# Layer 1's output stores issued from ScalarE, its loads alone on SyncE's queue, and eight matrix buffers

## The chip, the core and the metric

The kernel runs on one core of a Trainium2 chip. A core has a matrix engine (TensorE, PE in the profile), three engines for elementwise work (VectorE or DVE, ScalarE or ACT, GpSimd or POOL) and SyncE (SP), which here only issues transfers between the chip's main memory and its on-chip memory. ScalarE can issue transfers too; each of the two has a queue of its own. [...]

The metric is the device time of one execution in microseconds (us). Before the change it is 4470.12 us, the median of three runs between 4469.93 and 4470.48.

## The reference, cut to what matters

Two layers follow each other. Layer 0 takes the image through two 2-D Fourier transforms, a mixing of channels and a 3x3 convolution; the change doesn't touch it. Layer 1 filters along the first image axis:

```python
def _L1_conv_ref(x, w_real, w_imag):            # x: (4, 256, 256, 64)
    trend = _moving_average(x, 25)              # along axis 1
    xf = jnp.fft.rfft(x - trend, axis=1)
    xs = xf[:, :128]
    ys = jnp.einsum('bmnc,cmk->bknc', xs, w_real + 1j * w_imag)
    yf = jnp.concatenate([ys, zeros], axis=1)
    return trend + jnp.fft.irfft(yf, n=256, axis=1)
```

All of this is linear along axis 1 and differs only by channel. So it is one 256x256 matrix for each of the 64 channels, applied to 4 images of 256x256 values. The kernel makes the 64 matrices early, beside the first stages of layer 0, and puts them in main memory (`m_d`).

## The kernel before

Layer 0 ends with its result in main memory (`x2_d`). Layer 1 then works in 16 steps: eight groups of eight channels (`c`), and in each group two halves of the batch (`b0`). I call such a step, eight channels of two images, a half group.

```python
CM, CO = 2, 2
BH = max(1, B // 2)                    # 2 images
# CG = 8 channels, N = 256, P = 128, SW = 16

def x2_load(pool, c, b0, bufs):        # four loads of 1024 KB
    xc = pool.tile([P, 2, BH, N // SW, CG, SW], F32, tag="xc", name=..., bufs=bufs)
    for b in range(BH):
        for t in range(2):
            nc.sync.dma_start(xc[:, t, b], x2_d[b0 + b, t * P : (t + 1) * P, c // CG])
    return xc

def matrix_load(pool, c):              # the matrices of two channels, 512 KB
    mt = pool.tile([P, CM, 2, N], F32, tag="mt", name=f"mt_{c}", bufs=6)
    nc.sync.dma_start(mt, m_d[c : c + CM].rearrange("c p t n -> p c t n"))
    return mt

def layer1(c, b0, mts, xc, pool):
    nf = BH * N
    for i in range(CG):
        if i % CO == 0:
            oc = pool.tile([P, 2, BH, CO, N], F32, tag="oc", name=..., bufs=2)
        for to in range(2):
            ps = bank(...)             # one of 8 PSUM banks
            for t in range(2):
                nc.tensor.matmul(ps[:, :nf],
                                 mts[i // CM][:, i % CM, t, to * P : (to + 1) * P],
                                 xc[:, t, :, :, i, :], start=t == 0, stop=t == 1)
            dst = oc[:, to, :, i % CO, :]
            src = ps[:, :nf].rearrange("p (b n) -> p b n", n=N)
            bias = b_fp[:, c + i : c + i + 1]
            if to:
                nc.scalar.activation(dst, src, AF.Identity, bias=bias)
            else:
                nc.vector.tensor_scalar(dst, src, bias, None, ALU.add)
        if i % CO == CO - 1:           # every second channel: four stores of 256 KB
            at = c + i + 1 - CO
            for to in range(2):
                for b in range(BH):
                    nc.sync.dma_start(
                        out[b0 + b, to * P : (to + 1) * P, at : at + CO, :], oc[:, to, b])
```

The bias `b_fp` is left over from layer 0 and is added here. The steps are called in this order, once layer 0 is done:

```python
with tc.tile_pool(name="seq", bufs=1, side="left", reuse_waits="tile") as seq:
    mts = [matrix_load(seq, c) for c in range(0, CG, CM)]
    xc = x2_load(seq, 0, 0, 1)
    ...                                # the rest of layer 0
    with tc.tile_pool(name="seq2", bufs=1, side="right", reuse_waits="tile") as seq2:
        for c in range(0, C, CG):
            if c:
                mts = [matrix_load(seq, c + i) for i in range(0, CG, CM)]
            for b0 in range(0, B, BH):
                if c or b0:
                    xc = x2_load(seq2, c, b0, 3)
                layer1(c, b0, mts, xc, seq)
```

The order on PE, DVE, ACT and POOL is the written one for compute instructions. Where the loads and stores stand among each other on an issuing engine is decided by the scheduling layer that builds the program, which puts a transfer where it expects its buffer or its data to be ready. The input tile `xc` has three buffers after the first, which has one of its own; the matrices have six, of which a half group uses four.

## Time and profile before

| | whole kernel | layer 1, from 4002.4 us on |
|---|---|---|
| time | 4471.8 us in the profile | 469.4 us |
| PE busy | 4355.5 us | 446.3 us |
| DVE busy | 3562.4 us | 96.1 us |
| ACT busy | 2508.7 us | 87.9 us |
| POOL busy | 2777.9 us | 0 |
| instructions on PE in layer 1 | | 1024 matmul records for 512 calls |
| loads of `xc`: 1024 KB, issue to landing | | 64, median 7.5 us |
| loads of `mt`: 512 KB | | 32, median 3.7 us |
| stores of `oc`: 256 KB | | 256, median 3.0 us |

A 32-bit matmul appears as two records. A record's own duration (592 ns) overlaps the next one's, since matmuls are pipelined; the busy time in the table is that of the engine and counts an overlap once. Busy time of the three elementwise engines is low in this stage, so none of them is near its limit there, but each can still hold up the others by waiting. Transfers are issued by SyncE alone: 0.33 to 1.46 us for the issue of one store, with a median of 0.415 us. The data moves on 16 DMA engines[...].

### The profile page before, as it was taken

To read this page: it belongs to the slowest core of one execution; us is meant where nothing else is said; L and a number is where in the kernel's file an instruction comes from. 1 tells how busy PE (TensorE), PEld (TensorE's weight loads), DVE (VectorE), ACT (ScalarE), POOL (GpSimd) and SP (SyncE) were. 2 spreads that over 40 slices of the span, in tenths; PEclk is the share of its full clock that TensorE was granted. 3 is DMA by queue.
4 is the path that set the end of the run, shared out by engine and by line. 5 is a ranking of instruction groups with operands and counts; after the bars stand their busy time and mean duration, and the time that the engine had idled before them with its cause. 6 is when DMAs were issued, how large, how long until landed. Compare 5 with 4: busy or idle time off the path is not lost.

```text
span 4471.8 us, 63546 instructions
## 1 busy us (share of the span) xinstructions
PE 4355.5 (97%) x22379; PEld 2222.1 (50%) x22379; DVE 3562.4 (80%) x5473; ACT 2508.7 (56%) x3694; POOL 2777.9 (62%) x1774
## 2 busy tenths in 40 slices
PE   7899999799999999999999999999999999999999
PEld 4454443355555555555555555555555555554444
DVE  7979999899999999999998777777778788852212
ACT  2338888666666666666666666666664344331111
POOL 6779998887777777877776555555554555520000
PEclk9999999899999999999999999999999999999999
DMA  6664556434444444444444333333335333339987
GB/s 185 202 191 141 156 156 177 128 113 133 134 134 135 134 123 137 119 134 134 135 135 125 98 102 106 99 95 109 108 90 166 98 95 104 92 97 328 329 315 264
DMA packets 757734, 655.02 MB, mean 146 GB/s; under 512 B 40269, under 2 KB 651551, under 8 KB 749096
## 3 DMA queue, kind: packets, MB, share of 16 engines
q1 hardware_dynamic: 757416, 650.95, 48.2%
q8 instruction: 179, 2.93, 0.3%
q14 instruction: 139, 1.14, 0.1%
HBM read 364.81 MB, written 286.00 MB: 146 GB/s over the span
## 4 chain that ended last, share of the span: by engine, by line
PE 87%; DVE 4%; POOL 3%; DMA 2%; ACT 2%; issue 1%; SPq 1%; DVEq 0%; POOLq 0%; ACTq 0%
PE ps_h_c L916 19%; PE ps_h_c L935 11%; PE ps_p L565 9%; PE ps_o L1200 9%; PE ps_z L618 5%; PE ps_u L667 5%; PE ps_f_c L991 5%; PE ps_x L541 5%; PE ps_s_c L833 5%; PE ps_y L436 4%; PE ps_ft_c L1012 3%; PE ps_t_c L870 3%; PE ps_zt L635 2%; DMA xc<-x_d 1%; PE ps_m L1120 1%
## 5 line engine op out<-in xcount | busy, mean ns | idle before, releaser
L594 POOL TENSOR_TENSOR g<-g 128x512 f32<-128x512 f32 (+1 forms) x520 | 737.1, 1430 | 519.7 <-ACT g L588 519.7
L916 PE MATMUL ps_h_c<-td_c,wc_main 128*128 128x512 f32 x2048 | 921.7, 593 | 0.0
L584 DVE TENSOR_TENSOR g<-ps_p,g 128x512 f32<-128x512 f32 x1040 | 692.7, 681 | 29.8 <-ACT g L579 11.8
L588 ACT ACTIVATE g<-g,b_fc 128x1024 f32<-128x1024 f32 (+1 forms) x520 | 586.4, 1148 | 181.4 <-DVE g L584 179.2
L230 POOL TENSOR_TENSOR rstd_c<-var_c,minus_half 128x16 f32<-128x16 f32 x128 | 372.0, 2906 | 466.6 <-DVE var_c L224 455.9
L579 ACT COPY g<-ps_p 128x512 f32<-128x512 f32 (+1 forms) x520 | 302.4, 583 | 453.4 <-PE ps_p L565 439.1
L916 PEld LDWEIGHTS ps_h_c<-td_c,wc_main 128*128 128x128 f32 x2048 | 369.1, 190 | 369.8 <-issue 303.0
L935 PEld LDWEIGHTS ps_h_c<-td_c,wc_half 64*128 64x128 f32 x4032 | 417.0, 187 | 244.4 <-issue 194.4
L565 PE MATMUL ps_p<-xs,wp 64*128 64x512 f32 (+1 forms) x2080 | 518.8, 603 | 7.4 <-ACT xs L556 7.4
L935 PE MATMUL ps_h_c<-td_c,wc_half 64*128 64x128 f32 (+1 forms) x4032 | 515.3, 392 | 4.3 <-POOL td_c L890 4.3
L1200 PE MATMUL ps_o<-xc,mt 128*128 128x512 f32 x1024 | 446.3, 598 | 18.5 <-DMA xc<-x_d 18.5
L230 POOL TENSOR_TENSOR rstd<-var,minus_half 128x16 f32<-128x16 f32 x128 | 383.7, 2998 | 86.6 <-DVE var L224 86.5
L967 DVE TENSOR_TENSOR h_c<-h_c,ps_h_c 128x512 f32<-128x512 f32 x512 | 317.4, 682 | 125.9 <-PE ps_h_c L935 125.8
L984 ACT ACTIVATE h_c<-h_c,b_conv 128x1024 f32<-128x1024 f32 x256 | 280.6, 1147 | 200.7 <-DVE h_c L980 200.5
L1214 DVE TENSOR_SCALAR oc<-ps_o,b_fp 128x512 f32<-128x512 f32 x128 | 96.1, 750 | 366.2 <-PE ps_o L1200 348.1
L430 POOL TENSOR_TENSOR xb<-xt 128x512 f32<-128x512 f32 x224 | 290.2, 1314 | 94.4 <-DVE xt L423 91.7
L960 DVE TENSOR_TENSOR h_c<-h_c,ps_h_c 128x512 f32<-128x512 f32 x256 | 175.8, 687 | 202.6 <-PE ps_h_c L935 198.6
L1200 PEld LDWEIGHTS ps_o<-xc,mt 128*128 128x128 f32 x1024 | 195.5, 192 | 268.6 <-issue 239.4
L541 PEld LDWEIGHTS ps_x<-tab,yb 128*64 128x64 f32 x4064 | 241.9, 138 | 129.8 <-issue 92.1
L618 PE MATMUL ps_z<-g,w_tp 128*64 128x512 f32 x1024 | 282.3, 613 | 22.1 <-POOL g L594 20.8
L1212 ACT ACTIVATE oc<-ps_o,b_fp 128x512 f32<-128x512 f32 x128 | 87.9, 687 | 378.2 <-PE ps_o L1200 239.2
L436 PE MATMUL ps_y<-xb,tab 128*64 128x512 f32 x1024 | 259.3, 612 | 26.9 <-POOL xb L430 26.1
(144 smaller groups left out, 7681.3 us busy)
## 6 DMA issues: line engine op xcount, KB each, us to landing
y_d<-yt SPq DMA_DIRECT2D x256, 256.0 KB, 2.5
yb<-y_d SPq DMA_DIRECT2D x256, 256.0 KB, 3.6
u_d<-ut SPq DMA_DIRECT2D x256, 256.0 KB, 4.1
x_c<-in_x_dram SPq DMA_DIRECT2D x128, 512.0 KB, 5.5
x_d<-st SPq DMA_DIRECT2D x128, 512.0 KB, 4.8
xc<-x_d SPq DMA_DIRECT2D x64, 1024.0 KB, 7.5
out_dram<-oc SPq DMA_DIRECT2D x256, 256.0 KB, 3.0
xt<-in_x_dram SPq DMA_DIRECT2D x504, 128.0 KB, 2.6
```

Of the source, the lines that this page charges most:

```text
L230: nc.gpsimd.tensor_tensor(rstd, var, minus_half.to_broadcast([P, n]), ALU.pow)
L436: nc.tensor.matmul(ps[i * C : (i + 1) * C], dh[:, m, i * C : (i + 1) * C], sums[j][:, i], start=True, stop=True,)
L541: nc.tensor.matmul(ps[r * C : (r + 1) * C, j * N + t * P : j * N + (t + 1) * P], blk[:, t, k, r * C : (r + 1) * C], tb[:, t, :], start=Tru ...
L565: nc.tensor.matmul(ps[:, :nf], wp[rows, cols], rhs[rows], start=True, stop=r == 1 or not pr["special"],)
L584: nc.vector.tensor_tensor(gt[:, i], re, gt[:, 1], op)
L588: nc.scalar.activation(g, g, AF.Gelu, bias=b_fc[:, half : half + 1])
L594: nc.gpsimd.tensor_tensor(g[:, 0], g[:, 0], g[:, 1], op)
L618: nc.tensor.matmul(ps[r * C : (r + 1) * C, :nf], w_tp, d[:, :nf], start=True, stop=True)
L916: nc.tensor.matmul(ps, wc_main[:, par, k, :], ts[(*j, k)].rearrange("p j i -> p (j i)"), start=True, stop=False,)
L935: nc.tensor.matmul(pss[k, par][:, s * P : (s + n) * P], wc_half[lo : lo + C, k, :], ts[(*at_q, k)][lo : lo + C, at : at + n, :].rearrange( ...
L967: nc.vector.tensor_tensor(g, g, m, (ALU.add, ALU.subtract)[r])
L1200: nc.tensor.matmul(ps[:, :nf], mts[i // CM][:, i % CM, t, to * P : (to + 1) * P], xc[:, t, :, :, i, :], start=t == 0, stop=t == 1,)
```

## The change

The four stores after every second channel are issued by ScalarE in place of SyncE, which leaves SyncE with the loads alone in this stage. The aim is that a load no longer stands behind a store that waits for its product. The matrices get eight buffers in place of six, so that all four tiles of the next group have a free buffer while the present group's four are in use.

```diff
     def matrix_load(pool, c):
-        mt = pool.tile([P, CM, 2, N], F32, tag="mt", name=f"mt_{c}", bufs=6)
+        mt = pool.tile([P, CM, 2, N], F32, tag="mt", name=f"mt_{c}", bufs=8)
         nc.sync.dma_start(mt, m_d[c : c + CM].rearrange("c p t n -> p c t n"))
         return mt
@@
                 for to in range(2):
                     for b in range(BH):
-                        nc.sync.dma_start(
+                        nc.scalar.dma_start(
                             out[b0 + b, to * P : (to + 1) * P, at : at + CO, :], oc[:, to, b]
                         )
```

## The prediction

> **What bounds the kernel now.** I first asked where layer 1 lies and what PE does in it. PE's timeline from 4002 us on (columns: start us, us, engine, line, operation, tiles, count, and in brackets the idle time before it with its releaser) shows blocks of matmuls parted by waits:

> ```profile
> 4002.42 28.49 PE L1200 MATMUL ps_o<-xc,mt 128*128 128x512 f32 x66
> 4033.30 27.70 PE L1200 MATMUL ps_o<-xc,mt 128*128 128x512 f32 x64 [2.39 <-DMA xc<-x_d]
> 4061.42 55.20 PE L1200 MATMUL ps_o<-xc,mt 128*128 128x512 f32 x128 [0.41 <-DMA xc<-x_d]
> ...
> 4234.01 55.17 PE L1200 MATMUL ps_o<-xc,mt 128*128 128x512 f32 x128 [1.58 <-DMA xc<-x_d]
> 4292.84 58.18 PE L1200 MATMUL ps_o<-xc,mt 128*128 128x512 f32 x128 [3.67 <-DMA xc<-x_d]
> 4353.18 56.87 PE L1200 MATMUL ps_o<-xc,mt 128*128 128x512 f32 x128 [2.15 <-DMA xc<-x_d]
> 4412.93 54.34 PE L1200 MATMUL ps_o<-xc,mt 128*128 128x512 f32 x126 [2.89 <-DMA xc<-x_d]
> ```

> Nothing but a late `xc` parts the blocks, nearly always ahead of a new group of eight channels. Inside a block PE runs at 55.2 us for 128 records, 431 ns each. Two blocks of 128 take 58.18 and 56.87 us. The busy time by stretches tells why (busy us and count of PE, granted clock, DMA share, GB/s):

> ```profile
> 4292.80:4300.00 7.20, 7.16 (x10) 0.58 0.70 284
> 4300.00:4343.00 43.00, 43.00 (x101) 1.00 0.85 305
> 4343.00:4353.00 10.00, 8.03 (x19) 1.00 0.94 348
> 4353.00:4358.00 5.00, 4.82 (x8) 0.66 0.95 342
> ```

> After these two waits PE had a granted clock of 0.58 for 7.2 us and 0.66 for 5 us, which costs (1-0.58)x7.2 = 3.0 and (1-0.66)x5 = 1.7 us: just what the two blocks are too long by.

> Next, why `xc` is late. The chain that ended last (start us, us, what) leads from the 3.67 us wait back:

> ```profile
> 4281.49 0.70 ACT oc L1212
> 4282.19 0.02 issue
> 4282.20 0.33 SPq L1219
> 4282.54 0.04 issue
> 4282.58 0.68 SPq L1219
> 4283.27 0.04 issue
> 4283.31 9.49 DMA xc<-x_d
> 4292.80 0.04 issue
> 4292.84 50.47 PE ps_o L1200 x110
> ```

> The load took 9.49 us, but it was issued only at 4283.3, when two stores ahead of it in SyncE's queue had got the product they waited for. It isn't the buffer that was missing. Last, the waits of layer 1 by total (us, times, longest), those of the engines and those of SyncE's queue:

> ```profile
> PE ps_o L1200 <- DMA xc<-x_d: 18.5, 8, 3.7
> ```

> ```profile
> SPq L1219 <- DVE oc L1214: 237.7, 64, 9.5
> ...
> SPq L1219 <- ACT oc L1212: 47.0, 63, 0.8
> ```

> For 285 of some 470 us SyncE stands at a store that waits for DVE or ACT, with loads behind it.

> [...]

> **The change part by part.**

> *Loads without stores ahead of them.* The order of the changed program on PE, DVE and POOL is the same as before. On SyncE the four loads of an `xc` now follow each other. They are held by a free buffer and by a rotation of eight completion semaphores, which both queues share: each transfer waits for the one eight places ahead of it. I followed these places for the group at channel 48. The last load of its first half waits for the third store of channels 38 and 39; the half that follows, 40 to 47 of images 0 and 1, has just begun then. Before, its last load stood behind all four stores of channels 44 and 45 of images 2 and 3; in the chain above such a load left at 4283.3 for a PE that ran dry at 4289.2, 5.9 us later. So now it is issued over 1.5 half groups, more than 40 us, ahead of use, and the slowest landing above is 9.49 us. Every one of the 8 waits should go: 18.5 us.

> *The clock after the waits.* With no waits PE shouldn't be slowed: 3.0 + 1.7 = 4.7 us. Counter-check: 1024 records at 431.3 ns are 441.7 us; layer 1's matmuls now run from 4002.4 to 4467.3, 464.9 us. The difference, 23.2, is 18.5 + 4.7.

> *ACT's added work.* Per two channels ACT has two evictions of 0.687 us, and now four issues. No issue by ACT is in this trace; I take SyncE's median of 0.415 us. That is 1.37 + 1.66 = 3.0 us of the 6.9 us that PE needs for two channels (16 records x 431 ns). It lies beside PE. The stores come after ACT's own eviction, which they need, so ACT isn't held up by DVE for long: DVE's part is due 1.7 us sooner.

> *Stores and buffers.* A store that lands late delays the eviction two tiles on, and PE only when all 8 PSUM banks are full, that is after 8 x 4 x 431 ns = 13.8 us. I put nothing for it in the sum but in the remainder below.

> *The eight matrix tiles.* `mt` costs PE 1.4 us of waits, on the weight loads, and these overlap. Two more of these loads (1 MB) go to about 3464 us, where DMA is busy 46% of the time. Nothing for either.

> *The end.* Now two of the last four stores leave right after DVE, and the other two after ACT's last eviction. Then all four leave after it, one by one: two more issues, 0.8 us, and 0.5 MB more to move at the end, 1.5 us at 350 GB/s, which partly overlap: +1.5 us.

> Sum: -18.5 - 4.7 + 1.5 = -21.7, or 4448.4 us. For small waits of the new kind I add 2.6 us, a choice: 4451 us.

> **The rivals.**

> *DMA becomes the bound.* A half group moves 4 x 1024 + 2 x 512 + 16 x 256 KB = 9.44 MB. In 27.6 us (64 records) that is 342 GB/s. The busiest whole half group before had 340 GB/s at a DMA share of 0.95, so the limit is about 340/0.95 = 358 GB/s. That is a margin of 5%, and it speaks for this rival; for the main way speaks that slices of 12 us reach 365. If two queues with mixed reads and writes got only 330 GB/s, a half group would take 28.6 us, and some 13 of them 13 us in all: 4464.

> *A new wait takes the place of the old.* ACT's stores can wait for a semaphore that a load holds[...]. ACT then evicts late. If a store took 15 us in place of 3.0, evictions would be 6 to 8 us late, still within the 13.8 us of the banks. Were PE stopped by 1 us in each of 16 half groups, the time would be 4464; by more than 1.4 us, there is nothing left of the gain. Places that I followed show such a wait met by a load issued at least 7 us earlier, which speaks against it.

> *The loads were going to be late anyway*, because `xc` has three buffers. Against this: the buffer of a load is free two half groups ahead of use. It would leave 4470.

> **Range and chances.** The best case is 4447: 23.2 us gained, and an end that costs nothing. DMA as the bound or 1 us per half group ends at 4464. I take 4446 to 4464. A gain of over 2% would be 89 us, and only 23 are there; a loss of over 2% would need waits of 5 us in each half group. Faster by over 2%: 0.01; within 2%: 0.98; slower by over 2%: 0.01.

> **What would show each step right or wrong.** Right: PE's timeline is one block from 4002 to about 4444, with no idle time put down to `xc`; granted clock 1.00 throughout; ACT's queue issues 256 stores near 0.4 us each; the DMA share is 0.9 or more until some 50 us ahead of the end, then falls sooner than before. Wrong: PE idle for DVE or ACT (banks not free), or ACT long idle for `xc` or `out`, means the second rival; waits for `xc` with a share near 1 and under 342 GB/s mean the first; a load of `xc` issued in the half group just ahead of its use means that the buffer or the rotation holds it. A tail from the last eviction to the end of over 6 us would break the last term.

## The result, and the profile after

The changed kernel takes 4448.65 us (median of six runs, 4448.23 to 4452.21) against 4470.30 us before: a ratio of 0.9952 with a 95% interval of 0.9939 to 0.9965. That lies in the predicted range and 2.4 us under the predicted 4451. In the two profiles 4471.8 us became 4447.0.

PE's timeline of the changed kernel, layer 1 alone, in the columns of the prediction:

```profile
3999.99 55.10 PE L1200 MATMUL ps_o<-xc,mt 128*128 128x512 f32 x128
4056.39 384.80 PE L1200 MATMUL ps_o<-xc,mt 128*128 128x512 f32 x896 [1.30 <-DVE oc L1214]
```

Nine blocks have become two. No wait for `xc` is left, and what parts the two is not a load: PE stood 1.30 us for a PSUM bank that DVE had not emptied (I call this move from a bank to the product tile `oc` an eviction). From the first matmul to the end of the last it is 441.2 us in place of 464.9. From there to the end of the program it is 4447.0 - 4441.2 = 5.8 us in place of 4471.8 - 4467.3 = 4.5. Together -22.4 us, which is the effect within layer 1; layer 1 also began 2.4 us sooner, at 4000.0. I put that down to layer 0, whose code the change leaves alone, and the medians, 21.7 us apart, don't need it. It isn't shown to be chance, though: in the profiles below layer 1 begins at 4003.0 in e1, where SyncE issues the stores among the loads as before, and at 3997.0 to 4000.8 in all the others.

The waits of layer 1 by total (us, times, longest), the engines' first and then those of SyncE's queue:

```profile
DVE oc L1214 <- DMA out_dram<-oc: 181.1, 33, 12.3
...
ACT oc L1212 <- DMA out_dram<-oc: 151.3, 28, 10.5
...
PE ps_o L1200 <- DVE oc L1214: 1.3, 1, 1.3
```

```profile
SPq L1180 <- DMA out_dram<-oc: 172.0, 29, 13.5
...
SPq L1180 <- PE ps_o L1200: 36.6, 6, 7.6
```

Two things are to be seen. SyncE still waits for stores, 172 us at the loads of `xc`: that is the rotation of eight semaphores, in which a load waits for a store to land (in this trace the 342 transfers from 4001 us on use eight semaphores, 42 or 43 times each, and SyncE and ScalarE both use every one). It no longer matters, because these loads stand early enough. The last one of all is issued at 4368.1, and its half group begins at about 4414. The other is a wait which the prediction had as a rival: DVE and ACT stand 332 us in sum for product tiles whose stores haven't landed. It was there before, with 128 us in sum. Most of it was ACT's, in short waits (before):

```profile
ACT oc L1212 <- DMA out_dram<-oc: 117.6, 42, 3.1
```

The chain through PE's stop leads to such a store (start us, us, what):

```profile
4041.82 13.64 DMA out_dram<-oc
...
4055.59 0.76 DVE oc L1214
```

DVE waited 12.7 us here. The view by total puts this one wait, and one of 11.9 us of ACT beside it, down to a load of `mt`, so they are not in the 332. The list of transfers on the page (KB each, median us from issue to landing) shows the late landings too:

```profile
xc<-x_d SPq DMA_DIRECT2D x64, 1024.0 KB, 8.6
out_dram<-oc ACTq DMA_DIRECT2D x256, 256.0 KB, 6.0
```

A store needs 6.0 us where it needed 3.0, and 13.8 at the worst. The busy time by stretches (PE, PEld, DVE, ACT, POOL, each with its count, then granted clock, DMA share, GB/s) tells when:

```profile
4002.00:4085.00 83.00, 81.70 (x191) 36.01 (x190) 15.69 (x22) 14.24 (x22) 0.00 (x0) 1.00 1.00 379
4085.00:4389.00 304.00, 304.00 (x709) 134.53 (x709) 66.14 (x91) 60.64 (x90) 0.00 (x0) 1.00 0.90 341
4389.00:4444.00 55.00, 52.19 (x122) 22.80 (x120) 11.27 (x15) 10.99 (x16) 0.00 (x0) 0.99 0.41 153
```

For 83 us DMA is full, a share of 1.00 of which SyncE's queue took 0.64 and ScalarE's 0.36: the twelve loads that fill the three `xc` buffers are issued by 4042, and the loads of the next group follow from 4048 on. After that it runs at 0.90, and in the last 55 us it has the stores alone. Before, its share in the same three stretches was 0.88, 0.89 and 0.83. The granted clock is 1.00 from 4000.0 to 4441.2, so it no longer falls while PE has work left.

### The profile page after: what moved, and what is told of

Its sections match the earlier page's. It is cut to its first block, busy times and chain, and to the rows that moved or that the text cites. A ratio compares the mean times of both kernels' runs of the same rounds, so it can differ in the third digit from the quotient of the medians.

```text
span 4447.0 us, 63373 instructions
## 1 busy us (share of the span) xinstructions
PE 4346.2 (98%) x22379; PEld 2219.4 (50%) x22379; DVE 3561.7 (80%) x5473; ACT 2505.2 (56%) x3694; POOL 2774.3 (62%) x1774
## 4 chain that ended last, share of the span: by engine, by line
PE 88%; DVE 5%; POOL 2%; DMA 2%; issue 1%; ACT 1%; SPq 1%; ACTq 0%; DVEq 0%; POOLq 0%
PE ps_h_c L916 19%; PE ps_h_c L935 11%; PE ps_p L565 10%; PE ps_o L1200 9%; PE ps_z L618 5%; PE ps_u L667 5%; PE ps_f_c L991 5%; PE ps_x L541 5%; PE ps_s_c L833 5%; PE ps_y L436 4%; PE ps_ft_c L1012 3%; PE ps_t_c L870 3%; PE ps_zt L635 2%; DMA out_dram<-oc 1%; PE ps_m L1120 1%
## 5 line engine op out<-in xcount | busy, mean ns | idle before, releaser
L1200 PE MATMUL ps_o<-xc,mt 128*128 128x512 f32 x1024 | 439.9, 592 | 1.3 <-DVE oc L1214 1.3
L1214 DVE TENSOR_SCALAR oc<-ps_o,b_fp 128x512 f32<-128x512 f32 x128 | 93.2, 749 | 345.4 <-DMA out_dram<-oc 181.1
L1200 PEld LDWEIGHTS ps_o<-xc,mt 128*128 128x128 f32 x1024 | 194.4, 190 | 246.1 <-issue 236.1
L1212 ACT ACTIVATE oc<-ps_o,b_fp 128x512 f32<-128x512 f32 x128 | 85.9, 686 | 356.6 <-PE ps_o L1200 171.0
```

Source lines behind the costliest of these rows:

```text
L1200: nc.tensor.matmul(ps[:, :nf], mts[i // CM][:, i % CM, t, to * P : (to + 1) * P], xc[:, t, :, :, i, :], start=t == 0, stop=t == 1,)
```

## The experiments

The theory is *order*: before the change a load was late because it stood in one queue behind stores that waited for their product. Of the 60 loads of `xc` from 4002 us on, 38 stood right behind a store of `oc` in SyncE's queue before the change, and none after it. Its rivals: *buffers* (the two more matrix tiles did it), *queues* (two issuers move more, or stores must not stand behind loads), *depth* (loads must be far ahead). The table has what the runs gave; "matmuls" is the time from layer 1's first matmul to the end of its last, "stops" is PE's idle time in it, "end" is the rest of the program, all from the profiles.

| kernel | median us | ratio to before (95%) | matmuls | stops | end |
|---|---|---|---|---|---|
| before | 4470.30 | | 464.9 | 18.5 | 4.5 |
| changed | 4448.65 | 0.9952 (0.9939 to 0.9965) | 441.2 | 1.3 | 5.8 |
| e1 eight matrix tiles alone | 4460.66 | 0.9982 (0.9973 to 0.9991) | 452.9 | 10.1 | 4.5 |
| e2 stores on ScalarE alone | 4448.25 | 0.9949 (0.9936 to 0.9961) | 439.9 | 0 | 5.4 |
| e3 one queue, loads ahead | 4452.56 | 0.9955 (0.9943 to 0.9968) | 446.6 | 5.1 | 4.5 |
| e4 two input buffers | 4446.19 | 0.9948 (0.9936 to 0.9961) | 439.6 | 0 | 5.2 |
| e5 three product tiles | 4446.60 | 0.9954 (0.9942 to 0.9967) | 439.6 | 0 | 5.3 |
| e6 end split | 4446.11 | 0.9949 (0.9936 to 0.9962) | 440.0 | 0 | 4.7 |
| e7 stores on GpSimd | 4449.85 | 0.9959 (0.9946 to 0.9971) | 439.6 | 0 | 6.8 |
| e8 as e3, three product tiles | 4445.02 | 0.9950 (0.9936 to 0.9964) | 439.6 | 0 | 4.5 |
| e9 as e5, with e6's end | 4445.75 | 0.9944 (0.9930 to 0.9957) | 439.6 | 0 | 4.6 |
| e10 changed, again | 4448.73 | 0.9950 (0.9936 to 0.9965) | 440.4 | 0.5 | 5.8 |

Each ratio is to runs of the kernel before that were made beside it, whose medians went from 4467.05 to 4470.92; it can differ a little from the quotient of the two medians. The three terms come from one profile each. Where the runs can't tell two kernels apart, I compare these terms.

### e1: eight matrix tiles alone

```diff
# against the kernel before
-        mt = pool.tile([P, CM, 2, N], F32, tag="mt", name=f"mt_{c}", bufs=6)
+        mt = pool.tile([P, CM, 2, N], F32, tag="mt", name=f"mt_{c}", bufs=8)
```

> The kernel before with eight matrix tiles, all stores still on SyncE. Theory of order (a load stands behind stores that wait for their product): the loads of xc keep their places between the stores, so PE waits about 18 us for xc in 8 places and the time is that of before, 4470 us within 5. Rival of buffers (the free matrix tiles make the gain): 4449 us and no wait for xc.

Both missed: 4460.66 us, about halfway. The waits for `xc` fell from 18.5 to 10.1 us in six places. In PE's timeline (fifth and sixth block of seven):

```profile
4285.41 55.17 PE L1200 MATMUL ps_o<-xc,mt 128*128 128x512 f32 x128 [1.47 <-DMA xc<-x_d]
4343.22 56.87 PE L1200 MATMUL ps_o<-xc,mt 128*128 128x512 f32 x128 [2.64 <-DMA xc<-x_d]
```

Two of the eight waits are gone, those of 0.41 and 2.50 us. The six others stand at places that had a wait before. Four of them are much shorter (3.67 became 1.47 in the first line), and two are somewhat longer (2.39 became 2.77, and 2.15 became 2.64 in the second line). In this build a group's matrix loads all stand ahead of its first `xc` load. Before, two of them stood between the `xc` loads, 0.5 MB each in the last stretch ahead of the load that was due. In the chains that end in these waits the late load lands in 6.3 to 8.2 us, 7.3 in the mean of six, and before in 6.5 to 9.5, 7.9 in the mean of eight. That fits, and so does an earlier place of one group's last two loads; but no run varies one of them by itself. So that two more tiles take away part of the waits is shown (8.4 us by the runs, 12.0 by the two profiles); by which of the two ways is argued.

### e2: stores on ScalarE alone

```diff
# against the changed kernel
-        mt = pool.tile([P, CM, 2, N], F32, tag="mt", name=f"mt_{c}", bufs=8)
+        mt = pool.tile([P, CM, 2, N], F32, tag="mt", name=f"mt_{c}", bufs=6)
```

> Stores on ScalarE's queue, six matrix tiles as before. Theory of order: no wait of PE for xc, 441 to 444 us for layer 1's matmuls, 4449 us within 5. Rival of buffers: the third and fourth matrix tile of a group wait for a buffer until the half group ahead of use is under way and hold the loads of xc behind them, so PE waits for mt or xc by 5 to 20 us and the time is 4455 to 4468.

Order holds: one unbroken block.

```profile
3999.69 439.90 PE L1200 MATMUL ps_o<-xc,mt 128*128 128x512 f32 x1024
```

With e1 this makes a pair whose parts don't add up. The tiles alone brought 8.4 us, the queue alone 20.8 against the runs beside it, and both together 21.7: the tiles soften a wait that the queue takes away.

### e3: one queue, the loads ahead in it

```diff
# against the kernel before, with bufs=8 for mt
-                for c in range(0, C, CG):
-                    if c: mts = [matrix_load(...) ...]
-                    for b0 in range(0, B, BH):
-                        if c or b0: xc = x2_load(seq2, c, b0, 3)
-                        layer1(c, b0, mts, xc, seq)
+                fetch(1)                          # loads of half group 1
+                for k, (c, b0) in enumerate(steps):
+                    fetch(k + 2)                  # those of k + 2, ahead of k's stores
+                    layer1(c, b0, mtc[c], xcs[c, b0], seq)
```

> All transfers on SyncE, eight matrix tiles, but each half group's loads are asked for two half groups ahead in the source, so that on SyncE they stand together some six to eight sets of four stores ahead of use. Theory of order: one queue is enough, PE waits for xc fall from 18 us to under 3, and the time is 4450 to 4455 us. Rival of queues (two issuers move more bytes, or the stores must not stand behind the loads): PE still waits 10 us or more, for xc or for full banks, and the time is above 4460.

All transfers are SyncE's here, and no wait for `xc` is left. So a second queue isn't needed for that: place in the queue is the cause. Beside e1, which has the same eight matrix tiles and the same single queue, only the place of the loads differs, and 10.1 us of waits became none. The time, 4452.56, is in the range that order gave, but with one stop of another kind, which neither theory had in this form. The chain through it (start us, us, what):

```profile
4007.01 11.35 DMA xc<-x_d
4018.36 0.02 issue
4018.38 13.40 DMA out_dram<-oc
...
4031.96 0.69 ACT oc L1212
```

Eight loads of 1 MB stand ahead of the first stores. A store waits for a load in the rotation of semaphores, then lands in 13.4 us; ACT waits 17.4 us for the product tile, all 8 banks fill, and PE stops for 5.12 us. Two of the five runs took 4445.4 and 4446.4 us, as if without this stop; only one of the other three is profiled. The clock follows (busy us and count of PE, granted clock, DMA share, GB/s):

```profile
4027.00:4032.70 5.70, 0.58 (x3) 0.97 0.85 329
4032.70:4036.00 3.30, 3.30 (x4) 0.53 0.61 232
4036.00:4040.00 4.00, 4.00 (x11) 1.00 1.09 368
```

So a stop for a full bank can cost extra clock as one for a load does: (1-0.53)x3.3 = 1.6 us, where it was 1.7 after the stop of 2.15 us before.

### e4: two input buffers

```diff
# against the changed kernel
-                            xc = x2_load(seq2, c, b0, 3)
+                            xc = x2_load(seq2, c, b0, 2)
```

> The changed kernel with two buffers of xc in place of three (beside the first tile's own). A load is then issued at the start of the half group just ahead of its use, some 27 us ahead, and lands in 8 to 17 us. Theory of order: that is enough, no wait for xc, 4449 us within 4. Rival of depth (the gain needs loads more than one half group ahead): PE waits for xc, 1 to 3 us in each of some 14 half groups, and the time is 4463 to 4490.

Depth falls: no stop at all, 439.63 us of matmuls. A load one half group ahead is soon enough: it landed in 8.3 us (median), 12.9 at most. There isn't even the stop of 1.3 us; whether the four fewer loads at the start are the reason isn't shown, since e2 and e6 have no stop either with three buffers.

### e5: three product tiles

```diff
# against the changed kernel; the tiles lie in the other pool, which has the room
-                oc = pool.tile([P, 2, BH, CO, N], F32, tag="oc", name=..., bufs=2)
+                oc = pool.tile([P, 2, BH, CO, N], F32, tag="oc", name=..., bufs=3)
-                        layer1(c, b0, mts, xc, seq)
+                        layer1(c, b0, mts, xc, seq2)
```

> The changed kernel with three product tiles in place of two (kept in the other pool, where there is room). If the late evictions come from product tiles whose stores have not landed, a third tile gives a store some 7 us more: the waits of DVE and ACT for stores (181 and 151 us in the changed kernel) fall below 100 us in sum, PE has no stop for a full bank (1.3 us there), and the time is 4447 us within 3. Rival: the stores as such are too slow while loads run beside them; then a third tile only shifts the wait, the two sums stay above 250 us.

The waits for stores in this run:

```profile
ACT oc L1212 <- DMA out_dram<-oc: 97.5, 28, 5.2
DVE oc L1214 <- DMA out_dram<-oc: 42.1, 14, 4.2
```

From 332 us to 140, not quite under the 100 expected, and far from the 250 of the rival. The longest falls from 12.3 to 5.2 us, although a store still lands in 6.3 us (median). The stop is gone; but it was 1.3, 0.5 and 0 us in the changed kernel, e10 and e6, which have two product tiles and are alike up to the last stores, so one profile without it shows less than the waits do.

### e6: the end split between two issuers

```diff
# against the changed kernel
-                        nc.scalar.dma_start(
+                        last = at == C - CO and b0 == B - BH and to == 0
+                        (nc.sync if last else nc.scalar).dma_start(
```

> The changed kernel with two of its last four stores issued by SyncE, which has nothing left to do there. If the longer end (5.8 us from the last matmul to the end, 4.5 before the change) comes from four issues one after another on ScalarE, it falls to 4.5 us within 0.4, and the whole to 4447. If it comes from the bytes of the four stores, which leave late, it stays above 5.4.

The end is 4441.9 - 4437.2 = 4.7 us. Where its four stores go, in the summary of the transfers to the output (ns at least, median, at most; first and last start):

```profile
L1220 ACTq DMA_DIRECT2D out_dram<-oc x254: 338/447/2062, 4004.4 to 4438.4; - x127
L1220 SPq DMA_DIRECT2D out_dram<-oc x2: 338/386/433, 4436.3 to 4436.7; - x2
```

SyncE's two leave at 4436.3 and 4436.7, before ACT's last eviction at 4437.3. The longer end comes from the late start of these two. How much it is worth is less sure than one pair of profiles says: with all four on ScalarE the end was 5.2 to 5.8 us (the changed kernel, e2, e4, e5, e10), so the split saves 0.5 to 1.1. Whether the extra issues or the late bytes count for more isn't parted by this, since both go.

### e7: stores on GpSimd

```diff
# against the changed kernel
-                        nc.scalar.dma_start(
+                        nc.gpsimd.dma_start(
```

> The stores on GpSimd's queue in place of ScalarE's. Theory of order: it does not matter which engine issues the stores as long as it is not the one with the loads: no wait for xc, 440 to 443 us for layer 1's matmuls, 4449 us within 5. If ScalarE's four issues were what makes evictions late, ACT's waits for stores vanish here; if the landing of stores does, they stay near 150 us. Rival: GpSimd's issue is slower and holds the products longer, so PE stops for full banks by 5 us or more and the time is above 4455.

Order holds: 439.63 us in one block. The waits for stores stay at 178.5 us (DVE) and 123.1 (ACT), 302 us in sum where the changed kernel had 332, with ACT free of issues: what makes evictions late is in the main the landing, not ACT's issuing. GpSimd's issue takes 0.54 us (median; ScalarE's 0.444), and the end is longest here, 6.8 us.

### e8: one queue, three product tiles

```diff
# e3, with e5's change of the product tiles
-                oc = pool.tile(..., bufs=2)
+                oc = pool.tile(..., bufs=3)
```

> All transfers on SyncE with the loads asked for two half groups ahead, and three product tiles. The one stop of PE that was left with two (5.1 us, all 8 banks full in the first half group while eight loads stood ahead of the first stores) should shrink to under 1 us if the product tiles caused it: 4447 us within 4, and one queue is then as good as two. Rival: a single queue keeps a cost of its own, 4451 or more.

```profile
3997.04 439.63 PE L1200 MATMUL ps_o<-xc,mt 128*128 128x512 f32 x1024
```

The stop of e3 is gone, and one queue is as good as two: 4445.02 us with the short end, as SyncE sends the first of the last four stores at 4435.77, right after DVE's last eviction (4434.99 + 0.75) and before ACT's (4436.71).

### e9 and e10: both improvements, beside the changed kernel

```diff
# e9, against the changed kernel: e5 and e6 together
+                oc = pool.tile(..., bufs=3)
+                        (nc.sync if last else nc.scalar).dma_start(
```

> The changed kernel with both a third product tile and two of the last four stores on SyncE. Expected of layer 1: matmuls in one piece of 439.6 us, as with three products alone, and 4.5 us from the last matmul to the end, as with the end split alone: 1.6 + 1.2 = 2.8 us less than the changed kernel, 4446 us within 3. Rival: the two gains are one and the same, 4447.5 or more.

> The changed kernel beside it on the same chip: 4448.5 us within 3, matmuls of layer 1 over 441 us with a stop of 1 to 2 us for a full bank, 5.8 us within 0.4 from the last matmul to the end. If the stop is missing here, it is chance and not a property of the changed kernel.

e9 has the two terms as expected, 439.63 and 4.6 us, and 4445.75 us (4443.63 to 4447.50) beside 4448.73 (4445.67 to 4452.42) of e10. The medians differ by 3.0 us and the terms by 2.0 (440.4 + 5.8 against 439.6 + 4.6), but the ranges overlap and so do the intervals of the two ratios: by the times alone it isn't shown that e9 beats the changed kernel. e10's stop is 0.46 us. So PE stopped at this place in both profiles of the changed kernel, but not in that of e6, which is the same there: the stop is near its edge, and its length varies.

## Why the prediction was right

*Loads without stores ahead of them, -18.5 us: right, in mechanism and size.* All eight waits went. e1, e3 and e8 show that it is the place in the queue, since with one queue waits of 10.1 us are left when the loads stand among the stores, and none when they stand ahead; e4 shows that the 40 us of lead that I counted are more than is needed.

*The clock, -4.7 us: right.* PE's matmuls took 441.2 us with a stop of 1.3; the counter-check had said 441.7 without one. It was 2 us too high: an unbroken block of 1024 records takes 439.6 us, 429 ns each, and the 431 ns hold the last record's overlap (592 ns) of each block of 128. Where waits are left, as in e1 and e3, the clock still falls after some of them (2.64 us in e1) or after a stop for a bank (5.12 us in e3); that their place decides which ones is an inference (last section), so that the 4.7 us are those of the one profile before.

*ACT's issues lie beside PE: right.* The median issue was 0.444 us where I took 0.415, so ACT needs 3.1 us of the 6.9; e7 without them has nearly the same waits.

*Stores and buffers: nothing in the sum, 2.6 us for small waits of the new kind.* It measured 1.3 and 0.5 us. But the margin was much thinner than this suggests: I took evictions 6 to 8 us late as the bad case, and they waited up to 12.7 us where the banks give 13.8. These waits come one after another (DVE's of 12.3 and 12.7 us lie 4 us apart), so their lateness adds up: PE stopped after the second, while in e6 a wait of 13.9 us after one of 10.0 passed without a stop. That PE lost so little here was in part luck. e3 shows the other side of that edge. The rival named the right wait; it was hidden, not absent.

*The eight matrix tiles, nothing: right for the changed kernel* (e2 is as fast without them), *wrong for the kernel before* (e1). I had judged `mt` by PE's waits for it, 1.4 us, and overlooked that its loads share a queue with those that PE does wait for. Nor was DMA free where the two further loads go: the 46% that I gave are of 3460 to 3500 us, and from 3460 to 3468 the share was 0.99.

*The end, +1.5 us: right.* It measured 5.8 - 4.5 = +1.3, and +0.7 to +0.9 in e2, e4 and e5.

*DMA as the bound: the reason given was weak.* I scaled 340 GB/s at a share of 0.95 to a limit of 358. The changed kernel moved 379 GB/s for 83 us at a share of 1.00, and e8 moved 412 in the 27 us from 4005 on. The 330 GB/s for two queues was a supposition of mine, which no run shows. The rival had less behind it than I gave it; the upper end of my range, 4464, rested on it and on the second rival.

## What to carry to other kernels

When an engine waits for a load, compare the load's issue with its landing: if it is issued late, look at what stands ahead of it in its queue, and move it ahead of instructions that wait for results, by another queue or by order alone (18.5 us of waits here, none in e2 and e3). Once loads run ahead they can fill the DMA engines and make stores land later (here a share of 1.00 for 83 us in place of 0.88, and landings of 6.0 us in place of 3.0), so count how long evictions may be late (banks times the time to fill one, 13.8 us here) and give the products one tile more. Two fixes of the same wait don't add up (8.4 and 20.8 us alone, 21.7 together): test each alone.
